# Convolution results written over their inputs, and the inverse square root as a product of polynomials

## The chip, the core and the metric

The kernel runs on one core of one Trainium2 chip. The metric is the device time of one execution in microseconds. All data are 32-bit floats.

## What is computed

The reference has two layers on x of shape (4 images, 64 channels, 256, 256). The first is a long convolution with an implicit filter: per channel, a filter that is the outer product of two vectors of 256 taps, made by a small network of sines; the FFTs of size 512 make it a causal (not cyclic) convolution. Since the filter separates, it equals a Toeplitz product along the rows and one along the columns. The second layer takes the covariance of a ninth of the pixels over the channels, computes its inverse square root by five Newton-Schulz steps, and applies it to the centred image.

```
k = einsum('ijk,imk->ijmk', hx, hy)            # per channel: outer product of two 256-tap filters
y = irfft2(rfft2(x, 512) * rfft2(k, 512))[:256, :256] + x * bias

x1  = y as (64 channels, 4*256*256 pixels)
x1s = x1[:, ::9]
mean = mean(x1s, axis=-1)
cov = x1s @ x1s.T / n + 0.01 * I
Y, Z = cov / norm(cov), I
for _ in range(5):
    T = 0.5 * (3 I - Z @ Y);  Y = Y @ T;  Z = T @ Z
out = Z / sqrt(norm(cov)) @ (x1 - mean)
```

## The kernel before

*Set-up.* The filter taps are made on the chip in the first 20 us and written to DRAM (`g_d`). Toeplitz matrices are read back from there with overlapping rows into tiles `toep`, three buffers, one for each group of 8 channels.

*The convolution.* A step is a group of 8 channels (g) of one image (n); there are 32 steps. Steps 0 to 23 go through groups 0 to 5 with the four images inside; steps 24 to 31 go through the images, with groups 6 and 7 inside, so that image 0 is complete after step 25, image 1 after step 27, and so on. A step has four items of two channels (c = 0, 2, 4, 6). Each call of `group` (L381) interleaves the second Toeplitz product of an item with the first of the item two places later, four PSUM banks of eight; ScalarE moves the first product's result to SBUF (L396), VectorE makes `y = x * bias + second product` (L399) into a tile of its own, and SP stores it to DRAM (`store`, L407, 512 KB a store, rows of 1 KB). One call takes TensorE some 4.6 us; the calls are chained through two items (`pending`).

*Tiles.* One pool, `big`, holds three tiles of x (tag "in") and three of y (tag "out"), 2 MB each (16 KB per partition). x of step i+2 is loaded during step i (L103), one item's piece after each call of `group`.

*Sampling.* For every finished y tile, nine predicated copies on VectorE (L313) pick every ninth pixel into `samp[n]`, three copies after each call of `group`. The last half tile is picked by TensorE with selection matrices (`pack_by_pe`, L289). `covariance(n)` (L321) multiplies the samples of an image; that of image n-1 is taken in the middle of step (g=7, n), the last one after the convolution.

*The order.* The instructions of all engines stand in the order in which the program issues them (a manual schedule); a queue is served in that order. In particular, SP issues x loads, Toeplitz blocks, stores of y and reloads of y one after another, and each waits for what it needs while the others stand behind it.

*The second pass.* The whitening matrix W is applied to y, which comes back from DRAM in 32 pieces of 128 partitions x 4096 (2 MB). A piece holds 64 channels of two images (`pieces`, L338; `y_d` has 128 rows of one pair of images). A reload (`load_y`, L346) needs a free tile: 13 tiles become homes (L341): three of `toep`, four of `samp`, three of x and three of y. Eight reloads are issued inside the convolution, at the places that `early` (L372) names by step and item, five after it. A later piece waits until its home's earlier piece has been written out. Per 1024 columns: four matmuls (L585), two evictions on ScalarE (L590) and two on VectorE (L593) that add the shift, and an output DMA issued by POOL (L598), 2 MB each but for the first and last two pieces, which go in quarters.

*The inverse root.* Between the passes, on 64x64 matrices (L478 to L567): the norm as a square root on ScalarE with one correction step, then five rounds of ZY, T, YT, TZ. Each product goes through PSUM and is copied by VectorE (L505) or ScalarE (L550). At the end come the scaling, a product that doubles the matrix onto 128 partitions, and the shift `-W mean`.

Of the kernel before, what the change touches and what calls it, by code (L numbers as in the profile page):

```python
# [37 lines left out]
F32 = mybir.dt.float32  # L38
# [27 lines left out]
def conv_whiten_kernel(ctx: ExitStack, tc: tile.TileContext, a: dict, out: bass.AP):  # L66
# [4 lines left out]
    big = ctx.enter_context(tc.tile_pool(name="big", bufs=3))  # L71
# [6 lines left out]
    y_d = [dram.tile([2 * C, PIX], F32, tag=f"y{v}", name=f"y_d{v}") for v in range(NB // 2)]  # L78
# [5 lines left out]
    scratch = big.tile([P, 16, L], F32, tag="out", name="scratch")  # L84
# [14 lines left out]
    def new_x(g, n):  # L99
        return big.tile([P, CG, H2, L], F32, tag="in", name=f"x_{g}_{n}")  # L100

# [9 lines left out]
    loaded = {s: new_x(*s) for s in steps[:2]}  # L111
    for c in range(0, CG, 2):
        load_x(loaded[steps[0]], *steps[0], c)
# [147 lines left out]
    def half_group(item, which):  # L261

        g, n, c, xt, yt, o1s = item
# [11 lines left out]
        for m in range(H2):  # L275
            for u in range(2):
# [5 lines left out]
                else:  # L282
                    ch = g * CG + c + u
                    nc.vector.scalar_tensor_tensor(  # L284
                        yt[:, c + u, m], xt[:, c + u, m], bias[:, ch : ch + 1], ps,
# [35 lines left out]
    def covariance(n):  # L321
# [16 lines left out]
    pieces = [(v, q) for v in range(NB // 2) for q in range(PIX // FP)]  # L338
# [3 lines left out]
        {"t": (tpool, "toep"), "s": (spool, "samp"), "i": (big, "in"), "o": (big, "out")}[k]  # L342
        for k in "tssioitsoitos"
    ]

    def load_y(i):  # L346

        v, q = pieces[i]
        pool, tag = homes[i % len(homes)]
        t = pool.tile([P, FP], F32, tag=tag, name=f"yi_{v}_{q}")  # L350
        nc.sync.dma_start(out=t, in_=y_d[v][:, q * FP : (q + 1) * FP])
        return t
# [4 lines left out]
    loaded_x, loaded = loaded, {}  # L357
# [14 lines left out]
    early = {(28, 4): 1, (28, 6): 1, (29, 6): 1, (30, 4): 1, (31, 2): 1, (31, 4): 1, (31, 6): 2}  # L372
# [8 lines left out]
    def group(first, second):  # L381

        units = []
        g1, n1, c1, x1, _, o1s1 = first
        g2, n2, c2, x2, y2, o1s2 = second
# [7 lines left out]
        for u in range(2):  # L393
            o1 = o1pool.tile([P, H2, L], F32, tag="o1", name=f"o1_{g1}_{n1}_{c1 + u}")
            for to, fr in ((slice(0, HP), slice(HP, P)), (slice(HP, P), slice(0, HP))):
# [4 lines left out]
                y2[:, c2 + u], x2[:, c2 + u], bias[:, ch : ch + 1], units[u][1][0],  # L400
# [6 lines left out]
    def store(second):  # L407
        g, n, c, _, yt, _ = second
        last = (g, n) == steps[-1]
        row = n % 2 * C + g * CG + c  # L410
        nc.sync.dma_start(
            out=y_d[n // 2][row : row + 2, :].rearrange(
                "c (b p w) -> p (c b) w", p=P, w=L
            ),
            in_=yt[:, c : c + 2].rearrange("p c b w -> p (c b) w"),
        )
        if last and c == CG // 2 - 2 or not last and c == CG - 2:
            todo.extend(pack_ops(g, n, yt, slice(0, c + 2)))

    engines = mybir.EngineType  # L420
    with tc.manual_schedule(
# [7 lines left out]
        for c in range(0, CG, 2):  # L429
            load_x(loaded_x[steps[1]], *steps[1], c)  # L430
        for i, (g, n) in enumerate(steps):
            xt = loaded_x.pop((g, n))
            yt = big.tile([P, CG, H2, L], F32, tag="out", name=f"y_{g}_{n}")
            for c in range(0, CG, 2):
                item = (g, n, c, xt, yt, [])
# [7 lines left out]
                if i == 0 and c == 6:  # L443
# [3 lines left out]
                    twice = const.tile([C, 2, C], F32, tag="twice", name="twice")  # L447
                    for u in range(2):
                        nc.vector.tensor_copy(twice[:, u], ident[0:C, 0:C])

                part = (c - 2) // 2 % 4
                to = i + 2 if c else i + 1
                if to < len(steps) and to > 1:
                    if part == 0:
                        loaded_x[steps[to]] = new_x(*steps[to])
                    load_x(loaded_x[steps[to]], *steps[to], 2 * part)
# [8 lines left out]
        g, n, c, xt, yt, _ = pending[0]  # L465
# [4 lines left out]

        pack()
        pack_by_pe(g, n, yt, slice(CG // 2, CG))
# [3 lines left out]


    spare = {}  # L478
    for i in range(2):
        t = o1pool.tile([P, H2 * L], F32, tag="o1", name=f"chain{i}")  # L480
        for j in range(5):
            spare[5 * i + j] = t[0:C, 72 * j + 72 : 72 * j + 72 + C]
    ones = spare[9]
    nc.gpsimd.memset(ones, 1.0)  # L484
    i15 = spare[8]
    nc.vector.tensor_scalar(i15, ident[0:C, 0:C], 1.5, None, ALU.mult)
    spots = {"A": [0], "sq": [1], "Y": [2, 3], "T": [4, 5], "Z": [6, 7], "Zs": [1]}

    columns = [t[0:C, 440 + k : 441 + k] for k in range(H2 * L - 440)]

    def column():
        return columns.pop()

    def matrix(tag):
        spots[tag].append(spots[tag].pop(0))
        return spare[spots[tag][-1]]

    def product(lhsT, rhs, name):
        p = psA.tile([lhsT.shape[1], rhs.shape[1]], F32, tag="psA", name=name)
        nc.tensor.matmul(p, lhsT=lhsT, rhs=rhs, start=True, stop=True)  # L500
        return p

    def keep(p, name, tag):
        t = matrix(tag)
        nc.vector.tensor_copy(t, p)  # L505
        return t


    pd = product(fold, cov, "pd")
    A = matrix("A")  # L510
    nc.vector.scalar_tensor_tensor(A, ident[0:C, 0:C], EPS, pd[:, 0:C], ALU.mult, ALU.add)
    mean = column()
    nc.scalar.copy(mean, pd[:, C : C + 1])

    def root(v, name):

        s0 = column()
        nc.scalar.activation(s0, v, AF.Sqrt)  # L518
        r = column()
        nc.vector.reciprocal(r, s0)  # L520
        s1 = column()
# [135 lines left out]
```

## Time and profile before

| | us |
|---|---|
| median of 3 runs (917.23 to 919.46) | 918.35 |
| the profiled execution | 917.19 |
| its span, first to last instruction | 915.2 |
| TensorE busy | 789.1 (86%) |
| VectorE busy | 658.2 (72%) |
| ScalarE busy | 479.2 (52%) |
| POOL busy | 31.7 (3%) |

DMA moves 285.57 MB: x in, y out, y in and the result out are 67 MB each, the rest are Toeplitz blocks and small inputs. The mean granted TensorE clock was 0.946 of full speed. The page cuts the span into 40 slices of 22.9 us; a digit in a row is the busy share of a slice in tenths. The durations in the groups are of one instruction in ns; "idle before" is the time in which the engine stood still just before instructions of that group, with what ended it.

### The profile page before, as it was taken

How to read it: one execution, taken by the hardware profiler on the slowest of the kernel's cores; microseconds unless marked ns; L12 is line 12 of the kernel's file. 1: busy time of each engine (PE TensorE's matmuls, PEld its weight loads, DVE VectorE, ACT ScalarE, POOL GpSimd, SP SyncE). 2: the span in 40 equal slices, each digit the busy share in tenths (PEclk: the TensorE clock that was granted, in tenths of full speed). 3: DMA queues.
4: the chain of work that ended last, by engine and by line, in shares of the span. 5: the costliest groups of instructions: out<-in, count | busy, mean ns of one | idle time of the engine just before them, and what ended most of it. 6: DMA issues, size and time to landing. Idle time of an engine off the chain costs nothing.

```text
span 915.2 us, 27979 instructions
## 1 busy us (share of the span) xinstructions
PE 789.1 (86%) x11876; PEld 633.3 (69%) x11876; DVE 658.2 (72%) x882; ACT 479.2 (52%) x791; POOL 31.7 (3%) x71
## 2 busy tenths in 40 slices
PE   8999999999999999999999999997877777765500
PEld 7999999999999999999999999996311111111100
DVE  3468776877687768786878666867599999986500
ACT  2545454545454545454545444540498888866400
POOL 3000000000000000000000000000110000000010
PEclk9999999999999999999999999998699999987655
DMA  4988888798888888889997769989999999999998
GB/s 152 304 282 260 248 259 271 229 273 261 246 263 261 246 260 260 257 249 279 278 274 232 236 192 364 326 276 406 416 404 431 428 430 430 430 430 430 429 433 347
DMA packets 115499, 285.57 MB, mean 312 GB/s; under 512 B 6925, under 2 KB 89264, under 8 KB 107696
## 3 DMA queue, kind: packets, MB, share of 16 engines
q1 hardware_dynamic: 108176, 216.08, 71.0%
q0 software_dynamic: 6336, 67.11, 17.3%
q8 instruction: 94, 1.54, 0.7%
q10 hardware_dynamic: 864, 0.60, 0.2%
q14 instruction: 29, 0.24, 0.1%
HBM read 149.35 MB, written 134.42 MB: 310 GB/s over the span
## 4 chain that ended last, share of the span: by engine, by line
PE 68%; issue 15%; DVE 13%; DMA 1%; POOL 1%; ACT 0%; ACTq 0%; POOLq 0%; DVEq 0%
PE p L215 63%; DVE yi L593 12%; PE pc L327 2%; PE ph L247 1%; PE pk L295 1%; DMA mask<-in_mask_dram 1%; POOL pick L131 1%; PE po L585 1%; POOL out_dram L598 0%; DMA toep<-g_d 0%; DVE y L284 0%; PE ZY L500 0%; PE YT L500 0%; ACT L518 0%; DMA g_d<-scratch 0%
## 5 line engine op out<-in xcount | busy, mean ns | idle before, releaser
L215 PE MATMUL p<-toep,o 64*64 64x64 f32 (+3 forms) x5040 | 578.5, 284 | 0.2 <-issue 0.2
L215 PE MATMUL p<-toep,x 64*64 64x64 f32 (+3 forms) x5040 | 578.5, 284 | 0.1
L215 PEld LDWEIGHTS p<-toep,x 64*128 64x128 f32 (+1 forms) x5040 | 533.9, 166 | 23.4 <-issue 0.3
L215 PEld LDWEIGHTS p<-toep,o 64*128 64x128 f32 (+1 forms) x5040 | 535.2, 166 | 10.7 <-issue 0.4
L396 ACT COPY o<-p 64x512 f32<-64x512 f32 x504 | 292.4, 580 | 297.7 <-PE p L215 289.9
L313 DVE COPY_PREDICATED samp<-mask,y 128x448 f32<-128x448 int32 (+3 forms) x288 | 281.2, 976 | 6.6
L399 DVE SCALAR_TENSOR_TENSOR y<-x,bias,p 128x512 f32<-128x512 f32 x252 | 177.4, 743 | 138.7 <-PE p L215 138.1
L593 DVE TENSOR_SCALAR yi<-po,shift 64x512 f32<-64x512 f32 x256 | 192.0, 750 | 24.8 <-PE po L585 18.5
L585 PE MATMUL po<-yi,W 64*64 64x512 f32 x1024 | 152.4, 668 | 62.4 <-DVE yi L593 39.4
L590 ACT ACTIVATE yi<-po,shift 64x512 f32<-64x512 f32 x256 | 174.9, 683 | 43.9 <-PE po L585 36.8
L585 PEld LDWEIGHTS po<-yi,W 64*64 64x64 f32 x1024 | 36.8, 145 | 177.2 <-DVE yi L593 123.3
L598 POOL DMA_DIRECT2D out_dram<-yi x44 | 23.6, 537 | 263.2 <-DMA out_dram<-yi 115.4
L484 POOL MEMSET chain<- 64x64 f32 x1 | 0.1, 144 | 603.2 <-PE ph L247 603.2
L327 PEld LDWEIGHTS pc<-samp 128*64 128x64 f32 x464 | 14.3, 137 | 1.8 <-issue 1.0
L327 PE MATMUL pc<-samp 128*64 128x65 f32 x464 | 14.9, 223 | 0.4 <-ACT samp L304 0.4
L150 PE MATMUL busy<-idle 128*128 128x128 f32 x94 | 13.0, 301 | 0.0
L150 PEld LDWEIGHTS busy<-idle 128*128 128x128 f32 x94 | 12.4, 216 | 0.2 <-issue 0.2
L281 DVE COPY o<-ph 64x256 f32<-64x256 f32 x8 | 3.4, 421 | 9.1 <-PE ph L247 8.9
L295 PE MATMUL pk<-y,pick 128*128 128x112 f32 (+1 forms) x36 | 7.7, 388 | 2.6 <-DVE y L284 2.6
L335 DVE SCALAR_TENSOR_TENSOR cov<-pc,cov 128x65 f32<-128x65 f32 x4 | 0.9, 227 | 12.1 <-PE pc L327 12.1
L295 PEld LDWEIGHTS pk<-y,pick 128*128 128x128 f32 x36 | 7.2, 258 | 2.8 <-issue 2.7
L281 ACT COPY o<-ph 64x256 f32<-64x256 f32 x8 | 2.9, 367 | 10.0 <-PE ph L247 9.9
(81 smaller groups left out, 80.3 us busy)
## 6 DMA issues: line engine op xcount, KB each, us to landing
x<-in_x_dram SPq DMA_DIRECT2D x128, 512.0 KB, 5.5
y_d<-y SPq DMA_DIRECT2D x128, 512.0 KB, 4.2
yi<-y_d SPq DMA_DIRECT2D x32, 2048.0 KB, 16.4
out_dram<-yi POOLq DMA_DIRECT2D x28, 2048.0 KB, 44.3
out_dram<-yi POOLq DMA_DIRECT2D x16, 512.0 KB, 9.8
toep<-g_d SPq DMA_DIRECT2D x29, 256.0 KB, 6.6
toep<-g_d SPq DMA_DIRECT2D x29, 192.0 KB, 5.8
toep<-g_d SPq DMA_DIRECT2D x6, 128.0 KB, 3.2
```

Source lines behind the costliest of these rows:

```text
L131: nc.gpsimd.tensor_scalar(pick[:, s, :], ident, rows[:, s : s + 1], None, ALU.mult)
L150: nc.tensor.matmul(p, lhsT=idle[:, 0:P], rhs=idle[:, P : 2 * P], start=True, stop=True)
L215: mm = nc.tensor.matmul(ps[q : q + w, m, HP * k : L], lhsT=src[parts, k // 2, m * P + q : m * P + q + w], rhs=t[parts, : stop : -1] if k e ...
L295: nc.tensor.matmul(pk[:, b, :, 0:nj], lhsT=pick[:, (s - b) % STEP, :], rhs=yt[:, cs, b, s : s + STEP * (nj - 1) + 1 : STEP], start=(s == 0 ...
L313: nc.vector.copy_predicated(dst, m, src)
L327: nc.tensor.matmul(pc[half], lhsT=samp[n][:, b, j, 0:C], rhs=samp[n][:, b, j, :], start=(b == 0 and j < 2), stop=(b == H2 - 1 and j >= NJ ...
L396: nc.scalar.copy(o1[to], units[u][0][0][fr])
L399: nc.vector.scalar_tensor_tensor(y2[:, c2 + u], x2[:, c2 + u], bias[:, ch : ch + 1], units[u][1][0], ALU.mult, ALU.add,)
L585: nc.tensor.matmul(po[u][halves[k]], lhsT=W[halves[u]], rhs=yt[halves[u], cols[k]], start=True, stop=True,)
L590: nc.scalar.activation(yt[halves[0], cols[k]], po[0][halves[k]], AF.Identity, bias=shift[halves[k]])
L593: nc.vector.tensor_scalar(yt[halves[1], cols[k]], po[1][halves[k]], shift[halves[k]], None, ALU.add)
L598: nc.gpsimd.dma_start(out=o[:, end - part : end], in_=yt[:, end - part : end])
```

## The change

1. y is written over x (`scalar_tensor_tensor` with the same tile as input and output). Four fixed tiles (`x_tiles`) take the steps in turn, by `place_of`; from step 27 on only three are used. Two more tiles (`epool`) are free after the set-up. There are still 13 homes: two extra, four of x, three of `toep`, four of `samp`.
2. A tile can be loaded anew only when its y has been stored and sampled. x of step i+2 is loaded during step i up to step 24, from item c=0 on (before: from c=2 on); in step 25 nothing is loaded; from step 26 on, step i loads x of step i+1.
3. `y_d` has one tensor for each image, with rows of half a channel: (2 halves x 64 channels) x 32768. A store of an item becomes two stores of 256 KB. A piece is of one image, with both halves of the channels on the 128 partitions; the result has the same layout, and the host puts the axes in order.
4. Nine reloads are issued inside the convolution, from step 26 on; four after it.
5. The inverse root: with A the covariance and r = 1/norm(A), T0 = 1.5 I - 0.5 r A; the following factors are worked out from powers of A (A squared and cubed on TensorE while the norm is made), then per round Q = T T, M' = Q M, T' = 1.5 I - 0.5 M', and Z is multiplied up on the side with the mean as a 65th column. The last factor is made twice side by side, so that the last product comes out on 128 partitions and gives W and the shift at once. The square-root table is loaded by a dummy instruction in step 0.
6. Fill matmuls (`spin`): six after the last convolution product, seven while the norm is made, two after each of the products of the rounds.

```diff
-    big = ctx.enter_context(tc.tile_pool(name="big", bufs=3))
+    xpool = ctx.enter_context(tc.tile_pool(name="xpool", bufs=4))
+    epool = ctx.enter_context(tc.tile_pool(name="epool", bufs=2))
-    y_d = [dram.tile([2 * C, PIX], F32, tag=f"y{v}", name=f"y_d{v}") for v in range(NB // 2)]
+    y_d = [dram.tile([H2 * C, PIX // H2], F32, tag=f"y{n}", name=f"y_d{n}") for n in range(NB)]
...
+    x_tiles = {
+        u: xpool.tile([P, CG, H2, L], F32, tag="in", name=f"x{u}") for u in (3, 2, 0, 1)
+    }
+    def place_of(i):
+        return i % 4 if i < 27 else i % 3
...
-    pieces = [(v, q) for v in range(NB // 2) for q in range(PIX // FP)]
+    pieces = [(n, q) for n in range(NB) for q in range(PIX // H2 // FP)]
-        for k in "tssioitsoitos"
+        for k in "eeitssistiits"
...
-    early = {(28, 4): 1, (28, 6): 1, (29, 6): 1, (30, 4): 1, (31, 2): 1, (31, 4): 1, (31, 6): 2}
+    early = {
+        (26, 4): 1, (26, 6): 1, (27, 0): 1, (27, 2): 1, (27, 6): 1, (29, 6): 1, (31, 0): 1, (31, 4): 2
+    }
...
             nc.vector.scalar_tensor_tensor(
-                y2[:, c2 + u], x2[:, c2 + u], bias[:, ch : ch + 1], units[u][1][0],
+                x2[:, c2 + u], x2[:, c2 + u], bias[:, ch : ch + 1], units[u][1][0],
                 ALU.mult, ALU.add,
             )
...
-        row = n % 2 * C + g * CG + c
-        nc.sync.dma_start(
-            out=y_d[n // 2][row : row + 2, :].rearrange("c (b p w) -> p (c b) w", p=P, w=L),
-            in_=yt[:, c : c + 2].rearrange("p c b w -> p (c b) w"),
-        )
+        for b in range(H2):
+            row = b * C + g * CG + c
+            nc.sync.dma_start(
+                out=y_d[n][row : row + 2, :].rearrange("c (p w) -> p c w", w=L),
+                in_=yt[:, c : c + 2, b],
+            )
...
-                part = (c - 2) // 2 % 4
-                to = i + 2 if c else i + 1
-                if to < len(steps) and to > 1:
-                    if part == 0:
-                        loaded_x[steps[to]] = new_x(*steps[to])
-                    load_x(loaded_x[steps[to]], *steps[to], 2 * part)
+                to = i + 2 if i < 25 else i + 1
+                if i != 25 and to < len(steps):
+                    load_x(x_tiles[place_of(to)], *steps[to], c)
...
+    def spin(times):
+        p = psA.tile([P, P], F32, tag="psA", name=f"spin{len(spins)}")
+        spins.append(p)
+        for _ in range(times):
+            nc.tensor.matmul(p, lhsT=ident, rhs=ident, start=True, stop=True)
...
+    def whitening(i15, ones):
+        one_i15 = i15[:, 0]
+        pd = product(fold, cov, "pd")
+        A = place(C, rows=C)
+        nc.vector.scalar_tensor_tensor(A, ident[0:C, 0:C], EPS, pd[:, 0:C], ALU.mult, ALU.add)
...
+        pa2 = product(A, A, "pa2")
+        pn = product(ones, sq, "pn")
...
+        nc.vector.tensor_reduce(ssq, pn, AX.X, ALU.add)
+        nc.scalar.activation(s0, ssq, AF.Sqrt)
...
+        pa3 = product(A2a, A, "pa3")
+        spin(7)
...
+        nc.vector.scalar_tensor_tensor(U, pa3, rn_c, A2b, ALU.mult, ALU.add)
+        nc.vector.scalar_tensor_tensor(V, U, rn_c, A1b, ALU.mult, ALU.add)
+        T, M, Z = Ts[0], Ms[0], Zs[0]
+        nc.vector.scalar_tensor_tensor(T, V, rn_c, one_i15, ALU.mult, ALU.add)
+        nc.vector.tensor_scalar(M, V, rn_c, -2.0, ALU.mult, ALU.mult)
...
+        for k in range(1, N_ITER - 1):
+            pq = product(T, T, f"pq{k}")
+            if before is not None:
+                next_z(k - 1, before)
+            spin(2)
+            Q = Qs[k % 2]
+            nc.vector.tensor_copy(Q, pq)
+            pm = product(Q, M, f"pm_{k}")
...
+            if k < N_ITER - 2:
+                spin(2)
+                T, M = Ts[k % 2], Ms[k % 2]
+                nc.vector.scalar_tensor_tensor(T, pm, -0.5, one_i15, ALU.mult, ALU.add)
+                nc.vector.tensor_copy(M, pm)
...
+            else:
+                next_z(k, T)
+                spin(2)
...
+        pw = product(T, Z, "pw")
+        W = place(C)
+        nc.vector.tensor_scalar(W, pw[:, 0:C], rs, None, ALU.mult)
+        nc.scalar.activation(shift, pw[:, C : C + 1], AF.Copy, scale=nrs)
...
+        spin(6)
         pack()
...
+        W, shift = whitening(i15, ones)
```

`place` hands out columns of the tiles of the pool `o1`, and `product` is a matmul into a PSUM tile of its own.

## The prediction

> **What bounds the kernel now.** I read the page first: the 40 slices, then the costliest groups.
>
> ```profile
> span 915.2 us, 27979 instructions
> ...
> PEclk9999999999999999999999999998699999987655
> DMA  4988888798888888889997769989999999999998
> GB/s 152 304 282 260 248 259 271 229 273 261 246 263 261 246 260 260 257 249 279 278 274 232 236 192 364 326 276 406 416 404 431 428 430 430 430 430 430 429 433 347
> ...
> L215 PE MATMUL p<-toep,x 64*64 64x64 f32 (+3 forms) x5040 | 578.5, 284 | 0.1
> ```
>
> A slice is 22.9 us. Up to slice 26 (some 620 us) TensorE runs the Toeplitz products back to back: the row's last field, its idle time, is 0.1 us. Here DMA moves some 250 GB/s and has room. From slice 27 on, DMA stands at 430 GB/s, a ceiling. The second view is the table of stretches (columns: PE, PEld, DVE, ACT, POOL busy, granted clock, DMA share, GB/s).
>
> ```profile
> 512.00:545.00 33.00, 33.00 (x614) 30.84 (x613) 23.88 (x30) 15.56 (x28) 0.00 (x0) 1.00 0.65 207
> 554.10:572.90 18.80, 18.80 (x410) 17.69 (x408) 11.02 (x15) 7.12 (x13) 0.00 (x0) 1.00 0.99 390
> 604.00:616.00 12.00, 12.00 (x248) 11.39 (x244) 5.08 (x7) 3.70 (x7) 0.00 (x0) 1.00 0.89 289
> 616.00:912.50 296.50, 176.65 (x1273) 57.75 (x1270) 212.48 (x310) 179.29 (x268) 23.78 (x45) 0.84 1.00 422
> 621.70:625.10 3.40, 0.83 (x6) 0.58 (x5) 3.40 (x8) 0.00 (x0) 0.00 (x0) 1.00 1.13 448
> 625.10:628.50 3.40, 3.40 (x18) 3.40 (x17) 3.23 (x6) 0.00 (x0) 0.00 (x0) 0.51 0.99 424
> ```
>
> The fourth line decides: from 616 us to 912.5 us, DMA is at share 1.00, with no hole where the inverse root is computed (632 to 650 us). Third, the timeline there:
>
> ```profile
> 624.49 7.65 PE L295 MATMUL pk<-y,pick 128*128 128x116 f32 x36 [2.57 <-DVE y L284]
> ...
> 632.54 3.71 PE L327 MATMUL pc<-samp 128*64 128x65 f32 x116 [0.40 <-ACT samp L304]
> ...
> 650.10 6.49 PE L585 MATMUL po<-yi,W 64*64 64x512 f32 x29
> ...
> 654.34 0.73 POOL L598 DMA_DIRECT2D out_dram<-yi  x1 [35.48 <-PE po L585]
> ```
>
> The first output leaves at 654.3 us, yet DMA is busy throughout: five reloads of y (2 MB each) are issued between 625.65 and 639.4 us, and queue. So two things set the end: when TensorE finishes the convolution, and how many bytes are left for DMA then. The inverse root is covered by DMA.
>
> Last, the SP queue and its landing times (last column of the second fence: us from issue to landing; one issue per line, in the order 509.26, 549.70, 554.93, 558.83, 563.45):
>
> ```profile
> 509.26 0.50 SPq L103 DMA_DIRECT2D x<-in_x_dram  x1
> ...
> 549.70 0.50 SPq L103 DMA_DIRECT2D x<-in_x_dram  x1
> 550.30 0.87 SPq L351 DMA_DIRECT2D yi<-y_d  x1
> ...
> 554.93 0.43 SPq L351 DMA_DIRECT2D yi<-y_d  x1
> ```
>
> ```profile
> x<-in_x_dram SPq DMA_DIRECT2D x1, 512.0 KB, 5.7
> ...
> x<-in_x_dram SPq DMA_DIRECT2D x1, 512.0 KB, 5.8
> ...
> yi<-y_d SPq DMA_DIRECT2D x1, 2048.0 KB, 13.9
> ...
> x<-in_x_dram SPq DMA_DIRECT2D x1, 512.0 KB, 12.6
> ...
> x<-in_x_dram SPq DMA_DIRECT2D x1, 512.0 KB, 10.8
> ```
>
> Landings come in order of issue: 555.5, 568.8, 571.4, 574.3 us. The queue is first in, first out, so an x load behind two reloads takes 12.6 us in place of 5.8.
>
> **The change, part by part.**
>
> *1. y in the place of x; pieces of one image.* The 128x512 multiply-add (743 ns) writes x's tile; sizes are unchanged, so 0. Two tiles are freed, and image 0 is complete after step 25, so reloads start at step 26 in place of 28. From the store times (a step of four groups lasts some 18.6 us) the reloads issued inside the convolution move from 550, 555, 577, 590, 604, 613, 617, 617 us to about 510, 514, 519, 523, 536, 577, 600, 613, 613. At 613 us, where DMA saturates, seven have landed and two are issued, against five and one: two reloads ahead. 2 x 2.097 MB at 430 GB/s = **-9.75 us** of saturated tail. That holds only if the queue stays fed until outputs start: nine reloads, the stores and the last four (issued at about 625.7, 632, 632, 636 us, behind the packing, the pick products and the covariance) at 5.3 us each keep DMA busy to about 651 us.
>
> *2. What the early reloads push aside.* From step 25 on, x is loaded one step ahead in place of two (three tiles are left), and four reloads are put into four consecutive groups. The x load behind them for step 28, c=4 has the bytes of 4 reloads, 4 stores and 4 x loads after the x load of 509.26 (landed 515.0): 12.58 MB. The rate of such a mix is in the trace: between the x landings 555.5 and 574.3 lie 2 reloads, 3 stores, 3 x loads, 7.34 MB in 18.8 us, 390 GB/s. It lands at 515.0 + 32.2 = 547.2; TensorE wants it at 543.5 (the store of the group before, 544.34, less 0.82, the distance from a group's end to its store at 557.59/558.41). **3.6 us late.** The load for step 29, c=0 comes 4.19 MB (10.7 us) later, at 557.9, wanted at 552.8: 5.1 late, of which 3.6 is already paid. A 3.6 us gap also costs clock (below): 3.4 us at half speed, 1.7 us. Together the larger of 5.1 and 3.6+1.7: **+5.3 us** on the convolution's end, and the whole tail shifts with it. Here the Trainium skill weighs against the change: "HBM Reference", Specifications (TRN2), gives 358 GB/s per core, though its text says that a core streaming alone does better. With 358 the delay would be 9.0 us, and the change worth nothing; the trace has 390 in just this mix, so I take that.
>
> *3. Stores in two halves, loads behind the packing.* 128 stores of 512 KB become 256 of 256 KB, each with the same 1 KB runs. SP spends 0.38 us an issue, so some 0.4 us more per group of 4.6 us, of which it uses 1 to 2. In a backed-up queue a 512 KB store adds some 1.4 us; I take the halves at 0.7. A load at c=0 now waits for the last packing of its tile (up to 3 x 0.98 us after the multiply-adds); a Toeplitz block or a store queued behind it on SP waits as long. Below step 26 the cover is two steps: 0. If halves were slower, DMA's room (share 0.65 from 512 to 545 us) covers it, except in the crowded steps, where 0.2 us each would add some 2 us to part 2; a gain has no room, as TensorE has no idle time there.
>
> *4. The inverse root.* Before: covariance in at 636.5, W at 649.3, first output 654.3, with the clock at 0.50 from 638.7. After: six fill matmuls (0.28 us each, the row of L150) shorten the idle 2.57 us to 0.9; the pick products then run at full clock, but the last packings on DVE (to 631.5 us) allow only 0.7 us of gain. A square-root table load (1.28 us, about 0.5 of it exposed) moves to step 0, where ACT idles 1.5 us per group. Four rounds of three products become three of two squarings in the critical chain, but TensorE also runs the fills in order: a round is 2 products + 2 x 2 fills + side products, about 1.9 us at full clock. W at some 645.7, first output at 648.4: 6 us earlier. **Yet part 1's queue is busy to 651 us, so it is worth 0.** It is needed: with the old chain, DMA would idle some 3 us. The clock: "TensorE: Matmul & The Clock Gate", Part 1, puts the drop to half after an idle window of about 3.4 us. The trace dropped it after an idle gap of only 2.57 us (rows 621.7 and 625.1, with 0.83 us of TensorE work in the first). By the page the old gap did no harm and the fills there buy nothing; by the row they hold the clock. I follow the row. If the clock were half all the same, the fills (0.55 us each) would stretch the rounds to 3.7 us and the first output to some 656: +5 us.
>
> *5. Restart of the tail.* Between the end of the backlog and the first reload into a freed tile, DMA has only outputs (2.1 MB per 6.19 us, 339 GB/s). Before it ran at 349 to 419 GB/s there; I take **+0.5 us**.
>
> **Sum:** -9.75 + 5.3 + 0.5 = -4.0 us. The profiled execution was 917.19 us (span 915.2 and 2.0 around it), 1.2 under the median of 918.35; the difference is set against the median: **914.4 us**, a span of about 911.3.
>
> **The rivals.**
> - *The x loads come in time.* At the tail's 430 GB/s the two loads are 0.8 and 1.2 us late: -9.75 + 1.2 + 0.5, 910.3 us. For it: 430 is what the engines can do. Against it: 390 with 1 KB stores mixed in.
> - *Slower: the reloads starve TensorE in steps 28 and 29.* Five reloads, six stores and six x loads, 16.8 MB, must pass from 515.0 on. Delay passes 11.1 us (-9.75 + 11.1 + 0.5, the 0.2% bound) when they run under 344 GB/s; at 330 the delay is 13.1 us, 922.2 us. For it: a lone reload takes 9.2 to 9.6 us, and the stretch 604 to 616 gave 289 GB/s. Against it: 390 with two in the queue.
> - *The clock falls in the chain* (part 4): +1.0 us in all, 919.4, no change.
> - *The shorter chain is what counts* (if DMA were not full): -4.0 would be -6 or better. Against it: share 1.00 from 616 us.
>
> **How the numbers follow.** A measurement here tells about 0.2% (1.8 us) from no change. Main case 0.40 (911 to 917), no stall 0.22, cold chain or a delay of 7.5 to 11 us 0.17, starved 0.16, something unseen that costs 0.05. Range for 8 in 10: 908.0 (close to no stall) to 921.5. Faster 0.62, same 0.17, slower 0.21.
>
> **What would show it.** TensorE's Toeplitz products should wait for x in steps 28 to 29 (some 5 us, DMA as releaser), and the granted clock may dip at 547 us; before step 26, nothing. The first output should leave near 653 us (648.4 + 5.3), with DMA at share 1.0 from about 618 us on, and 13 reloads issued by then. Wrong: no wait for x (then near 910), a wait over 11 us, DMA idle before the first output, or clock 0.5 in the chain.

## The result, and the profile after

| | before | after |
|---|---|---|
| median | 917.17 us (915.12 to 919.46) | 917.69 us (915.40 to 920.36) |
| span of the profiled execution | 915.2 us | 915.7 us |
| end of the last Toeplitz product | 621.9 us | 628.3 us |
| first output issued | 654.34 us | 656.88 us |
| mean granted clock | 0.946 | 0.957 |

The ratio is 0.9997, with a 95% interval of 0.9988 to 1.0007: no change that can be measured. (The 917.17 us are of 12 runs beside those of the changed kernel; the 918.35 us from which the forecast started were of three.) The forecast was 914.4 us; the time lies inside the range, but "faster" was the likeliest outcome and did not come. That the range holds is partly luck: an unchanged time was forecast only with a clock of 0.5 in the chain or a delay of 7.5 to 11 us, and neither came.

The rows of the page of the changed kernel that answer to those shown of before:

```profile
span 915.7 us, 28266 instructions
...
PEclk9999999999999999999999999999999999996655
DMA  4988778788788788878984899789999999999998
GB/s 154 298 282 273 253 243 262 256 258 259 258 261 264 237 266 265 262 236 267 291 277 138 302 412 340 252 286 357 379 379 432 426 432 429 429 432 429 429 433 340
...
L220 PE MATMUL p<-toep,x 64*64 64x64 f32 (+3 forms) x5040 | 580.8, 285 | 3.8 <-DMA x<-in_x_dram 3.1
```

Three things are new. In slices 22 and 23 (counted from 0; 504 to 550 us) DMA moves 302 and 412 GB/s where it moved 236 and 192: the early reloads. In slice 21, just before, it moves 138 GB/s in place of 232: in step 25 no x is loaded. And the Toeplitz products now have idle time, 3.1 us of it ended by a load of x. In slices 27 to 29 (618 to 687 us) the GB/s row reads 357, 379, 379 where it read 406, 416, 404: DMA has holes where it was full.

The stall, in the timeline of TensorE and then in the table of stretches (columns: PE, PEld, DVE, ACT, POOL busy, granted clock, DMA share, GB/s):

```profile
540.99 0.24 PE L220 MATMUL p<-toep,x 64*64 64x64 f32 x1 [0.34 <-DMA x<-in_x_dram]
548.53 0.45 PE L220 MATMUL p<-toep,x 64*128 64x256 f32 x1 [2.74 <-DMA x<-in_x_dram]
```

```profile
541.00:548.00 7.00, 4.80 (x78) 4.19 (x78) 5.11 (x7) 4.11 (x8) 0.00 (x0) 1.00 1.00 393
548.30:549.70 1.40, 1.17 (x9) 1.07 (x11) 0.00 (x0) 0.00 (x0) 0.00 (x0) 0.99 1.17 469
549.70:553.10 3.40, 3.40 (x22) 3.12 (x20) 0.00 (x0) 0.00 (x0) 0.00 (x0) 0.50 1.03 439
553.10:560.00 6.90, 6.90 (x139) 6.51 (x137) 4.90 (x6) 3.26 (x6) 0.00 (x0) 1.00 1.01 386
```

An x load that came 2.74 us late, then 3.4 us at clock 0.50, half of which (1.7 us) is my estimate of the further cost. The first multiply-add of each group stands 1.5 us later than before at step 27, c=2, 2.1 us at c=6, and 7.2 us one group on: 5.7 us in all, 5.1 of them in one place. At the end of the convolution 6.4 us are left; some 1.4 us of that is spread over the first 26 steps, and not every profile shows it.

Now the tail. For each kernel the stretch in which DMA can run out of work, up to 668 us, with parts of it, and the stretch from 616 us to the end of the span. Before, then after:

```profile
616.00:632.00 16.00, 13.43 (x99) 12.55 (x96) 15.15 (x26) 1.41 (x3) 0.14 (x1) 0.89 1.01 399
656.00:668.00 12.00, 11.90 (x85) 3.44 (x77) 11.62 (x17) 11.68 (x18) 3.70 (x7) 1.00 1.00 399
616.00:668.00 52.00, 42.02 (x358) 26.21 (x355) 35.50 (x75) 19.22 (x34) 4.61 (x9) 0.80 1.01 410
616.00:915.20 299.20, 176.65 (x1273) 57.75 (x1270) 212.48 (x310) 179.29 (x268) 23.78 (x45) 0.83 0.99 419
```

```profile
616.00:632.00 16.00, 14.97 (x213) 13.83 (x210) 14.25 (x21) 4.64 (x8) 0.20 (x1) 1.00 0.88 322
648.00:656.00 8.00, 7.62 (x64) 5.02 (x65) 3.38 (x14) 2.38 (x7) 0.00 (x0) 1.00 1.01 430
656.00:668.00 12.00, 11.86 (x78) 3.34 (x70) 11.62 (x17) 11.66 (x19) 4.20 (x8) 1.00 0.77 291
616.00:668.00 52.00, 48.96 (x526) 35.42 (x522) 38.68 (x79) 19.99 (x40) 4.39 (x9) 1.00 0.92 358
616.00:915.70 299.70, 185.13 (x1452) 66.22 (x1448) 217.87 (x317) 181.92 (x276) 23.90 (x45) 0.87 0.98 409
```

These lines give the whole balance. Rate times length of the longer stretch is what DMA still had to move at 616 us: 125.4 MB before, 122.6 MB after, so 2.8 MB less, worth 6.5 us at 430 GB/s. Rate under 430 from 616 to 668 us is what it failed to move: 20 x 52 = 1.0 MB (2.4 us) before, 72 x 52 = 3.7 MB (8.7 us) after. So 6.5 us of head start were won and 6.3 us of holes were added. The added holes lie in two places of about the same size. From 616 to 632 us, while the delayed convolution still runs (to 628.3 us), the rate is 322 GB/s against 399: 1.2 MB, 2.9 us. From 656 us on, where the first outputs leave and DMA has little else, it is 291 against 399: 1.3 MB, 3.0 us. In between DMA is nearly full, at 430 GB/s from 648 to 656 us, up to just before the first output (656.88 us).

The chain between the passes, in the timeline of TensorE of the changed kernel:

```profile
630.98 7.60 PE L300 MATMUL pk<-x,pick 128*128 128x116 f32 x36 [1.03 <-DVE x L289]
638.98 3.71 PE L332 MATMUL pc<-samp 128*64 128x65 f32 x116 [0.40 <-ACT samp L309]
643.01 0.33 PE L448 MATMUL pd<-cov,fold 128*64 128x65 f32 x2 [0.32 <-DVE cov L340]
...
652.64 0.43 PE L448 MATMUL pw<-chain,chain 64*128 64x65 f32 x2
653.45 7.00 PE L622 MATMUL po<-yi,chain 64*64 64x512 f32 x56 [0.38 <-DVE chain L541]
```

From the convolution's end to the first output it takes 28.5 us where before it took 32.4. The clock stayed at 1.00 there, so the new root did what it says; it started 6.4 us later.

How far the backlog of reloads reaches past the first output is read from the issue of the last of the 13 reloads, its time to landing, and the issue of the first reload into a freed tile (first and third line from the timeline of SP, the second from the list of transfers). Before, then after:

```profile
638.08 1.31 SPq L351 DMA_DIRECT2D yi<-y_d  x1
yi<-y_d SPq DMA_DIRECT2D x1, 2048.0 KB, 25.5
668.16 0.32 SPq L351 DMA_DIRECT2D yi<-y_d  x1
```

```profile
642.73 0.32 SPq L356 DMA_DIRECT2D yi<-y_d  x1
yi<-y_d SPq DMA_DIRECT2D x1, 2048.0 KB, 15.8
664.80 0.32 SPq L356 DMA_DIRECT2D yi<-y_d  x1
```

Before, the last reload landed at 663.6 us, 9.3 us after the first output was issued. After, it landed at 658.5 us, 1.6 us after the first output. I call this the lead of the backlog.

### The profile page after: what moved, and what is told of

Its sections match the earlier page's. It is cut to its first block, busy times and chain, and to the rows that moved or that the text cites. A ratio compares the mean times of both kernels' runs of the same rounds, so it can differ in the third digit from the quotient of the medians.

```text
span 915.7 us, 28266 instructions
## 1 busy us (share of the span) xinstructions
PE 793.6 (87%) x11922; PEld 637.6 (70%) x11922; DVE 658.8 (72%) x882; ACT 480.1 (52%) x796; POOL 31.9 (3%) x71
## 4 chain that ended last, share of the span: by engine, by line
PE 68%; DVE 17%; issue 7%; DMA 5%; ACT 1%; POOL 0%; POOLq 0%; DVEq 0%; ACTq 0%; SPq 0%
PE p L220 62%; DVE yi L630 16%; DMA yi<-y_d 3%; PE pc L332 2%; DMA x<-in_x_dram 1%; PE ph L252 1%; PE po L622 1%; PE pk L300 1%; PE spin L433 0%; ACT yi L627 0%; POOL out_dram L635 0%; DMA toep<-g_d 0%; DVE x L289 0%; DVE scratch L168 0%; ACT scratch L164 0%
## 5 line engine op out<-in xcount | busy, mean ns | idle before, releaser
L318 DVE COPY_PREDICATED samp<-mask,x 128x448 f32<-128x448 int32 (+3 forms) x288 | 281.2, 976 | 6.7
L406 DVE SCALAR_TENSOR_TENSOR x<-x,bias,p 128x512 f32<-128x512 f32 x252 | 177.4, 743 | 145.1 <-PE p L220 144.6
L622 PE MATMUL po<-yi,chain 64*64 64x512 f32 x1024 | 150.6, 655 | 60.7 <-DVE yi L630 42.3
L622 PEld LDWEIGHTS po<-yi,chain 64*64 64x64 f32 x1024 | 35.1, 141 | 175.2 <-DVE yi L630 131.6
L300 PE MATMUL pk<-x,pick 128*128 128x112 f32 (+1 forms) x36 | 7.6, 385 | 1.0 <-DVE x L289 1.0
L300 PEld LDWEIGHTS pk<-x,pick 128*128 128x128 f32 x36 | 7.1, 206 | 1.3 <-issue 1.2
```

Of the source, the lines that this page charges most:

```text
L300: nc.tensor.matmul(pk[:, b, :, 0:nj], lhsT=pick[:, (s - b) % STEP, :], rhs=yt[:, cs, b, s : s + STEP * (nj - 1) + 1 : STEP], start=(s == 0 ...
L318: nc.vector.copy_predicated(dst, m, src)
L406: nc.vector.scalar_tensor_tensor(x2[:, c2 + u], x2[:, c2 + u], bias[:, ch : ch + 1], units[u][1][0], ALU.mult, ALU.add,)
L622: nc.tensor.matmul(po[u][halves[k]], lhsT=W[halves[u]], rhs=yt[halves[u], cols[k]], start=True, stop=True,)
```

## The experiments

Theory: the head start of the reloads is real (some 9.7 us), but it is lost in two places: a stall of TensorE, because x loads queue behind four reloads, and a DMA queue that runs dry as the first outputs leave, so that the inverse root, hidden before, is on the path. Rivals: the stores in two halves or the writing over x cost time; the fill matmuls cost or save time; the tail restarts badly because the first reload into a freed tile comes late.

The times below stand against runs of the kernel before on the same chip (medians 917.75, 917.75 and 917.38 us in the three batches).

### Reloads spread out

At most one reload in two groups, otherwise the changed kernel; still nine inside the convolution.

```diff
-        (26, 4): 1, (26, 6): 1, (27, 0): 1, (27, 2): 1, (27, 6): 1, (29, 6): 1, (31, 0): 1, (31, 4): 2
+        (26, 4): 1, (27, 0): 1, (27, 4): 1, (28, 0): 1, (28, 4): 1, (29, 6): 1, (31, 0): 1, (31, 4): 2
```

> The changed kernel with the same nine early reloads, the first five moved apart: after (26,4), (27,0), (27,4), (28,0), (28,4) in place of (26,4), (26,6), (27,0), (27,2), (27,6). Theory (x loads stand behind a run of four reloads in the first-in-first-out queue): TensorE's wait for x in steps 28 and 29 (2.7 us and the half clock after it) goes, the convolution ends near 623.5 us in place of 628.3, the first output leaves near 652 in place of 656.9, and the time falls by 4 to 5 us against before (ratio 0.995). Rival 1 (the one-step lead, not the reloads, makes x late): the wait stays. Rival 2 (the lost time is DMA's at the start of the tail, so TensorE's wait costs nothing): the wait goes and the time stays at 1.000.

Measured: 911.19 us (910.92 to 912.86), ratio 0.9936 (0.9922 to 0.9949): 5.8 us faster than before by the ratio. The stretches of this kernel:

```profile
500.00:560.00 60.00, 60.00 (x1098) 56.39 (x1096) 43.76 (x54) 29.10 (x51) 0.00 (x0) 1.00 0.95 348
...
616.00:632.00 16.00, 15.00 (x114) 14.21 (x110) 15.56 (x27) 1.74 (x3) 0.20 (x1) 1.00 1.00 386
648.00:656.00 8.00, 8.00 (x62) 2.39 (x54) 7.29 (x10) 7.37 (x11) 2.33 (x4) 1.00 0.75 308
650.70:653.00 2.30, 2.30 (x21) 0.70 (x14) 2.24 (x4) 2.24 (x4) 1.24 (x2) 1.00 0.48 191
656.00:668.00 12.00, 10.28 (x66) 2.50 (x64) 11.63 (x17) 11.68 (x18) 2.44 (x5) 1.00 0.94 342
...
616.00:668.00 52.00, 47.41 (x428) 30.56 (x424) 40.11 (x82) 23.14 (x43) 4.98 (x10) 1.00 0.95 377
616.00:909.30 293.30, 178.54 (x1322) 60.71 (x1318) 213.24 (x312) 179.08 (x271) 23.91 (x45) 0.87 0.98 413
```

TensorE is busy for 60.00 of 60 us and the clock is 1.00: no stall, although x is loaded one step ahead here too. The convolution ends at 622.2 us, the first output leaves at 650.67. So the stall cost the changed kernel some 6 us: 5.6 by the two ratios, 6.5 by the medians (917.69 less 911.19), where the interval of this ratio alone is 2.5 us wide. At 616 us DMA had 121.1 MB left, 4.2 MB less than before: the two reloads of head start, with nothing taken off. Yet only 5.8 us of their 9.8 arrived, because the holes are 53 x 52 = 2.8 MB (6.4 us) against 2.4 us before: -9.8 + 4.0 = -5.8, and the spans differ by -5.9 (909.3 against 915.2). Of the two places, the first is nearly gone (386 GB/s from 616 to 632 us); the holes lie from 648 us on.

### Reloads at the old places

The changed kernel with the reload places of before: what do the layout, the half stores, the loads behind the packing and the new root bring without the head start?

```diff
-    early = {
-        (26, 4): 1, (26, 6): 1, (27, 0): 1, (27, 2): 1, (27, 6): 1, (29, 6): 1, (31, 0): 1, (31, 4): 2
-    }
+    early = {(28, 4): 1, (28, 6): 1, (29, 6): 1, (30, 4): 1, (31, 2): 1, (31, 4): 1, (31, 6): 2}
```

> The changed kernel with the early reloads at the places they had before: (28,4), (28,6), (29,6), (30,4), (31,2), (31,4) and two at (31,6). Theory: no wait for x, the convolution ends near 623 us; the tail has the bytes it had before, DMA is full through the inverse root, so the time is that of before within 1 us (1.000 to 1.001). If writing y over x or the stores in halves cost something by themselves, this run shows it: over 1.002. Rival (the shorter inverse root counts): 3 us less, 0.997.

Measured: 917.69 us (915.75 to 919.45), ratio 0.9999 (0.999 to 1.0007). No wait for x, the first output at 649.51 us (4.8 us earlier than before), and in its stretches DMA is full all through:

```profile
632.00:656.00 24.00, 22.53 (x253) 13.85 (x248) 13.75 (x40) 10.57 (x24) 2.73 (x5) 1.00 1.02 424
656.00:668.00 12.00, 9.88 (x69) 2.32 (x64) 11.64 (x16) 11.68 (x18) 2.27 (x5) 1.00 1.01 418
```

So half stores, the place of y and the later loads, together with the new root, change nothing that can be measured, and an earlier first output is worth nothing here. Parts of under a microsecond that cancel are not excluded.

### The new root alone, and the old root in the changed kernel

Two crossed kernels: the kernel before with the new root and the fills, and the changed kernel with the old root and no fills.

```diff
 # in the kernel before
-    (norm, five rounds of ZY, T, YT, TZ, doubling, shift)
+    spin(6); ...; W, shift = whitening(i15, ones)
 # in the changed kernel: the reverse
```

> The kernel before with only the new inverse root and its fill matmuls (parts 5 and 6 of the change). Theory: DMA is full from 616 us to the end, so the first output leaves some 4 us earlier (650 in place of 654.3) and the time stays: 1.000 within 0.1%. Rival (the inverse root is on the path): 3 to 4 us less, 0.996.

> The changed kernel with the old inverse root and no fills. Theory: here DMA ran dry at 656 us (217 GB/s from 656 to 660, 0.77 of its time from 656 to 668), so the later first output (about 660.7 in place of 656.9, by the 32.4 us from the end of the convolution to the first output before, against 28.5) is paid in full: 3 to 4 us slower than the changed kernel, 1.004 of before. Rival (covered by the reloads, as I predicted): 0.

Measured: the new root alone 916.99 us, ratio 0.9991 (0.9983 to 0.9999); the old root in the changed kernel 921.79 us, ratio 1.0044 (1.0031 to 1.0056). In the one the first output moved by -4.4 us (649.97) and the time by -0.8; in the other by +4.5 us (661.42) and the time by +4.1. The second kernel's tail:

```profile
656.00:668.00 12.00, 11.76 (x78) 4.22 (x78) 9.04 (x15) 8.57 (x13) 2.83 (x5) 0.84 0.49 197
```

At share 0.49, DMA idles for half of this stretch: the last of the 13 reloads landed at 659.7 us, before the first output was even issued. The same chain was hidden in the kernel before and is exposed in the changed one.

### No fills

```diff
     def spin(times):
-        p = psA.tile([P, P], F32, tag="psA", name=f"spin{len(spins)}")
-        spins.append(p)
-        for _ in range(times):
-            nc.tensor.matmul(p, lhsT=ident, rhs=ident, start=True, stop=True)
+        return
```

> The changed kernel without any fill matmul. Theory: the fills are what holds the granted clock at 1.0 in the chain; without them it falls to about 0.50 between the end of the convolution and the first output matmuls. The pick products take 7.6 us all the same (they took 7.65 us before with 3.4 us of them at half clock, and 7.60 us in the changed kernel at full clock), so they are not bound by the clock. The chain from covariance to W (10.4 us with fills) loses the waits behind fills and gains some 0.2 us a product: between 10 and 12 us. The first output moves by 0 to +1.5 us, and since DMA ran dry there, the time by about as much: 917.5 to 919, ratio 1.000 to 1.002. Rival (the prediction's cold chain): half clock costs 5 us, ratio 1.005 or more. Second rival: the fills cost more than the clock brings, ratio 0.998 or less.

Measured: 917.73 us, ratio 1.0 (0.9991 to 1.0008), the same as with fills. The stretches of the chain (pick products; chain to W; first outputs):

```profile
632.00:640.00 8.00, 7.60 (x38) 7.23 (x37) 6.60 (x13) 0.27 (x1) 0.00 (x0) 0.62 1.00 371
...
644.00:653.60 9.60, 5.47 (x30) 3.86 (x30) 5.12 (x27) 1.82 (x10) 0.00 (x0) 0.73 1.01 429
653.60:657.90 4.30, 4.26 (x20) 1.30 (x24) 1.98 (x3) 2.15 (x4) 0.00 (x0) 0.50 0.83 354
```

The clock does fall. The pick products take 7.91 us (7.60 with fills), and the first output matmuls take 4.3 us up to the first output (3.4 with fills). But the products of the rounds no longer stand behind fills: from `pd` to `pw` it takes 8.57 us (644.00 to 652.57) against 9.63. From the end of the convolution to the first output: 28.9 us without fills, 28.5 with. They hold the clock and give it back as queueing on TensorE.

### Quarter reloads into the first freed tiles

The first two reloads into freed tiles, in four parts, so that each waits for its own quarter's output alone; once in the changed kernel, once with spread reloads.

```diff
-            loaded[i + len(homes)] = load_y(i + len(homes))
+            if i < 2:
+                m, r = pieces[i + len(homes)]
+                for w in range(4):
+                    nc.sync.dma_start(
+                        out=yt[:, w * 1024 : (w + 1) * 1024],
+                        in_=y_d[m][:, r * FP + w * 1024 : r * FP + (w + 1) * 1024],
+                    )
+                loaded[i + len(homes)] = yt
+            else:
+                loaded[i + len(homes)] = load_y(i + len(homes))
```

> The changed kernel, with the first two reloads into freed tiles cut in four, so that each quarter waits for the output of its own quarter alone. Theory: from 656 to 668 us DMA lost 1.3 MB (291 GB/s against 399 before) because the first whole reload waits for four outputs; the quarters start after the first of them and fill some 0.7 to 1.3 MB of it: -1.6 to -3.0 us, ratio 0.9967 to 0.9983, 390 GB/s or more from 656 to 668 us. Rival: the tail is not bound by DMA there but by how soon outputs leave (VectorE and ScalarE are busy 97% in that stretch), so that bytes moved early only queue later: 0, ratio 0.9995 to 1.0005. Second rival: quarters on the SP queue delay each other and the whole reloads behind them: slower by up to 1 us.

> The kernel with spread reloads (911.2 us) and the first two reloads into freed tiles cut in four. Theory: there DMA moved 342 GB/s from 656 to 668 us and 368 from 640 to 656; the quarters fill the first of the two: -1.0 to -2.4 us against 911.2, 908.8 to 910.2 us, ratio 0.9910 to 0.9925. Rival (outputs bound the tail): 911 us, ratio 0.9936.

Measured: 916.84 us, ratio 0.9995 (0.9985 to 1.0004), and 912.15 us, ratio 0.9938 (0.9924 to 0.9953). Both miss. With spread reloads and quarters:

```profile
648.00:656.00 8.00, 8.00 (x65) 2.45 (x57) 6.80 (x10) 6.90 (x11) 2.10 (x4) 1.00 0.72 267
656.00:668.00 12.00, 10.04 (x65) 2.52 (x66) 11.59 (x16) 11.65 (x18) 2.37 (x5) 1.00 1.00 386
```

The quarters did start earlier (3.2 us after the first output, at 654.28 us, where the whole reload came 7.9 us after it) and filled the second stretch: 386 against 342 GB/s. The first stretch was no better, 267 against 308, so that over 616 to 668 us the rate is 379 against 377. Most of the hole (163 x 8 = 1.3 MB of 1.8 MB from 648 to 668 us) lies in the first stretch, where DMA waits for the first output and then has little but outputs; reloads issued from 654.28 us on come too late for it. The rivals of both expectations, with no gain from the quarters (0.9995 to 1.0005, and 0.9936), have the numbers right; their reason, that the pace of the outputs and not DMA sets the end there, was not tested.

### One fill in place of two

The kernel just above, with `spin(1)` for each `spin(2)`.

```diff
-            spin(2)
+            spin(1)
```

> As the one before, with one fill matmul in place of two after each product of the rounds. Theory: the products that stand behind the fills start up to 0.3 us earlier, five or six times: first output 1 to 1.5 us earlier, clock still 1.0; DMA had room there, so 0 to -1.2 us against the kernel before it. Rival: one fill is too few, the clock falls to 0.5 in the rounds, first output no earlier, time the same or up to 1 us more.

Measured: 911.97 us, ratio 0.9937 (0.9923 to 0.9951): no difference. From `pd` to `pw` it took 8.39 us in place of 9.63, as expected. But then the clock fell in the first output matmuls, which took 4.3 us in place of 3.4:

```profile
641.00:650.00 9.00, 7.84 (x60) 6.08 (x58) 5.12 (x27) 1.87 (x11) 0.00 (x0) 0.98 1.00 424
650.00:653.40 3.40, 3.40 (x20) 1.16 (x24) 1.25 (x2) 1.53 (x3) 0.00 (x0) 0.55 1.03 439
```

Most of the gain of the chain (1.2 us) went into these 3.4 us at clock 0.55 (0.9 us). Both sides of the expectation were right in part, and they cancelled to 0.3 us; the clock fell behind the rounds, not in them.

### One reload moved by one group

The prediction's arithmetic of the queue, tested: the x load that came late (step 28, c=4) stands behind three reloads in place of four.

```diff
-        (26, 4): 1, (26, 6): 1, (27, 0): 1, (27, 2): 1, (27, 6): 1, (29, 6): 1, (31, 0): 1, (31, 4): 2
+        (26, 4): 1, (26, 6): 1, (27, 0): 1, (27, 4): 1, (27, 6): 1, (29, 6): 1, (31, 0): 1, (31, 4): 2
```

> The changed kernel with one reload moved by one group, from step 27 c=2 to c=4, so that the x load of step 28 c=4 (issued 535.36, landed 548.4, waited for by 2.74 us) stands behind three reloads in place of four. By the prediction's arithmetic a reload is 5.4 us at 390 GB/s: that load comes in time, and the next ones, behind four, take over the stall. Theory: the following load (step 28 c=6) is then 1 to 3 us late: 2 to 4 us are won back of the 6.4: 914 to 916, ratio 0.996 to 0.998. Rival 1: the stall only moves (no gain): 917.5, ratio 0.9995 or more. Rival 2: three in a row are harmless, the stall is gone: 911 to 912, ratio 0.993 to 0.9945.

Measured: 917.77 us, ratio 1.0003 (0.9993 to 1.0013): nothing is won. Its waits of TensorE between 540 and 575 us, and the stretches:

```profile
PE p L220 <- DMA x<-in_x_dram: 3.3, 2, 2.6
```

```profile
552.00:556.00 4.00, 2.73 (x30) 2.19 (x26) 3.27 (x5) 1.96 (x4) 0.00 (x0) 1.00 0.97 372
556.00:560.00 4.00, 2.65 (x17) 2.68 (x19) 2.37 (x3) 0.36 (x1) 0.00 (x0) 0.79 1.06 398
560.00:564.00 4.00, 4.00 (x84) 3.88 (x85) 0.25 (x1) 0.15 (x1) 0.00 (x0) 0.79 0.95 362
```

The stall only moved: the jump of the multiply-adds against before stands two groups later (1.8 us at step 28, c=2, 6.8 us at c=4; in the changed kernel 2.1 to 7.2 us at c=0), 5.0 us in place of 5.1, with the dip of the clock behind it. The next two x loads stand behind the fourth and the fifth reload, and the prediction's order of bytes has the second of them, for step 29, c=0, late too. Behind three reloads the load came in time; room for the others has to be made by distance, as the spread kernel does.

### Part of the sampling left out

The pick products and the covariance of the last image left out, in three kernels: with spread reloads, as changed, and with the reloads at the old places. This was to bring the first output forward by some 12 us and so price the chain.

```diff
-        pack_by_pe(g, n, yt, slice(CG // 2, CG))
-        covariance(NB - 1)
```

> The kernel with spread reloads, without the pick products and the covariance of the last image (left out: the samples of the last half tile and of image 3 are missing from the whitening matrix); all else, the four last reloads too, is as there. Theory: with spread reloads DMA had 4.15 MB less to move at 616 us than before (9.65 us), but lost 7.0 us to holes up to 912 us against 3.7 before, 4.7 of them between 648 and 668 us, while it waited for the first outputs. With W some 12 us earlier (first output near 638.5) the backlog covers the whole chain and the holes from 648 to 668 go: -4 to -5 us against 911.2, 906 to 907.5, ratio 0.988 to 0.989. Rival: the holes are not due to the late first output (SP's queue, or the order of small and large transfers); then they stay and the time falls by less than 1 us, ratio 0.9925 to 0.994.

> The changed kernel, with the same part left out (pick products and covariance of the last image). Theory: its hole from 656 to 668 us (291 GB/s, 1.67 MB under 430) goes, as the first output leaves near 644.5 us: -3.5 to -4.5 us, 913 to 914, ratio 0.995 to 0.9965. The prediction's own view (the queue covers the inverse root): 0, ratio 0.9995 to 1.0005.

> The changed kernel with its reloads at the places of before (917.7 us), with the same part left out. Theory: there DMA was at share 1.01 through the whole chain (the backlog covers it), lost bytes from 616 to 700 us are 0.9 MB; the first output 12 us earlier is worth at most 1 us: 916.7 to 917.7, ratio 0.9989 to 1.0. Rival: the first output sets the end in every kernel: -4 us or more, ratio 0.996 or less.

Measured: 909.34 us, ratio 0.9912 (0.9896 to 0.9928); 914.94 us, ratio 0.9977 (0.9965 to 0.9988); 917.36 us, ratio 1.0002 (0.9993 to 1.0012). The edit did not do what it was meant to do. With spread reloads, TensorE then stood for one long wait:

```profile
PE pa L448 <- DVE chain L461: 8.0, 1, 8.0
```

VectorE still had its packings to do, and the chain's first operation (L461) stands behind them; in that wait the clock fell (0.61 from 628 to 640 us). So the first output came only 3.4 us earlier (647.32), and the time fell by 1.9 us (2.2 by the ratios, whose intervals just touch). The DMA stretch from 616 to 668 us reads 394 GB/s against 377:

```profile
632.00:656.00 24.00, 23.03 (x148) 12.67 (x148) 15.97 (x45) 12.71 (x27) 3.39 (x6) 0.89 1.01 424
...
616.00:668.00 52.00, 41.00 (x298) 22.60 (x294) 43.11 (x85) 26.70 (x48) 5.19 (x10) 0.90 1.00 394
```

That is 17 x 52 = 0.9 MB, 2.1 us, as much as the time fell. With the old places the first output came even later (652.85 against 649.51 us, at the lower clock), and the time did not change; but the landing of the last reload moved as far, so the lead of the backlog stayed (13.7 us against 13.2). In the kernel in the middle the time is 2.8 us under the changed kernel's (1.8 by the ratios), but its runs spread from 912.7 to 920.5 us and the profiled one, of 918.5 us, lies near their upper end (first output 657.96 us), so that its profile doesn't show where the median gained.

## Where the prediction was right, and the step that failed

The sum was -9.75 (head start) + 5.3 (stall) + 0.5 (restart) = -4.0 us. In the same terms the runs give -9.8, +5.6 to 6.5 and +4.0 us, together between -0.2 and +0.7; measured were -0.3 by the ratio and +0.5 by the medians. The first and the last term are read from the kernel with spread reloads, the stall is the difference between that kernel and the changed one. So nearly all that the forecast missed lies in the restart.

*Part 1, the head start: right.* 4.2 MB (9.8 us) less to move at 616 us, in the kernel with spread reloads, against 4.19 MB and 9.75 us predicted. In the changed kernel the stall leaves 2.8 MB of it.

*Part 2, the stall: right in its mechanism, and in size as far as can be told.* Which x load would be late, behind which bytes, and the dip of the clock came as worked out: 3.6 us late was forecast and 2.74 + 0.34 us came; the convolution slipped by 5.7 us there, against 5.3. Moving one reload moved the stall and won nothing. The rate was right too: 393 GB/s from 541 to 548 us. The 358 GB/s of the Trainium skill ("HBM Reference", Specifications (TRN2)) did not weigh against the change, as the prediction had it: the page gives them as a core's share while both cores of a pair stream, and this kernel has one core at work. The rivals on this part fell: "in time" by the wait, "starved" by its size.

*Part 3, half stores, y over x, loads behind the packing: right, 0 within what can be measured.* The kernel with the old places is 0.9999 of before.

*Parts 4 and 5: this step failed.* "Part 1's queue is busy to 651 us, so it is worth 0" took a queue that lasts until the first output as enough, and part 5 put the restart behind it at 0.5 us. In the kernel without a stall the times came close to the forecast: DMA was full to about 650 us (forecast 651), the first output left at 650.67 (forecast 648.4), and the last reload landed 1.6 us after it. Yet the holes cost 4.0 us more than before. Until the first reload into a freed tile, issued 7.9 us after the first output, DMA has little but outputs: 191 GB/s from 650.7 to 653 us, 342 from 656 to 668. The 349 to 419 GB/s that the prediction read for this phase in the kernel before were the rate of a covered restart: there the backlog had a lead of 9.3 us, and the outputs queued up with it. The reloads of the head start are that cover. Two reloads landed early are 9.75 us less of backlog to hide the chain and the restart behind, while the first output moved by only 3.7 us (654.34 to 650.67). The cause stands on pairs of kernels, in which a shift of the first output has different prices:

| pair | lead of the backlog | shift of the first output | change of the time |
|---|---|---|---|
| before, with the new root | 9.3, then 13.9 us | -4.4 us | -0.8 us |
| old places, part of the sampling left out | 13.2, then 13.7 us | +3.3 us | -0.3 us |
| changed kernel, with the old root | 1.6, then -1.7 us | +4.5 us | +4.1 us |
| spread, part of the sampling left out | 1.6, then 5.6 us | -3.4 us | -1.9 us |

With a lead of 9 us and more, an earlier first output brings next to nothing (first row). With one under 6 us, a microsecond of chain costs between a half and a whole one (third and fourth row). The second row agrees but is no test, since the lead did not change. The forecast had noted that the new root "is needed" and that with the old chain DMA would idle some 3 us (the old chain cost 4.1). The rival "the shorter chain is what counts" was right in its mechanism, but not as it was put: the chain counts in the changed kernel because the cover is gone, which takes from the head start and adds nothing to -4. I take leads and shifts from one profile of each kernel, and in these profiles the convolution of like kernels ends up to 3.6 us apart, so the slopes are rough.

*The clock in the chain.* The fills hold it at 1.00, as forecast, but this is worth nothing: without them the time is the same, because each fill also stands in front of a product. The 0.7 us hoped for from the pick products did not come either: they take 7.60 us at full clock, as against 7.65 with 3.4 us of half clock. The Trainium skill ("TensorE: Matmul & The Clock Gate", Part 1) puts the drop after an idle window of some 3.4 us; here a gap of 2.74 us in the convolution was followed by 3.4 us at half clock, as one of 2.57 us was before. The row, not the page, was the right guide.

*The first output* was forecast near 653 us and came at 656.88: 648.4 + 5.3 against 650.67 + 6.2. So without the stall it was 2.3 us later than forecast. Some 1.2 us of that is the second fill: `pd` to `pw` takes 9.63 us with two fills after each product, 8.39 with one. The rest was not traced.

The best version of these runs is the spread one: 911.19 us, 0.9936 of before. Quarters and one fill on top of it brought nothing that can be measured.

## What to carry to other kernels

A transfer moved ahead of a saturated stretch buys its full time there only if the stretch stays saturated; the same bytes were hiding whatever ran beside them. So after every such step ask three things: when the backlog now ends, when the first work that feeds DMA again can leave, and when the transfers that wait for this work can start. Here a backlog that ended 1.6 us after the first output left holes worth 4 us more than one that ended 9.3 us after it. Price a microsecond of what lies between at a half to a whole one, not at zero. Early transfers in a first-in, first-out queue are best put apart, with the loads that the critical engine waits for between them: four in consecutive groups cost some 6 us, the same number at half the density none.

## What the runs showed that I had not expected

- The strided pick products are nearly independent of the clock: 7.60 us at 1.00, 7.65 us with 3.4 us of half clock, 7.91 us at a mean of 0.62. The output matmuls up to the first output are not: 3.4 against 4.3 us.
- Filling a hole in DMA with more eager reloads raised the rate from 656 to 668 us from 342 to 386 GB/s and yet left the sum to 668 us where it was (377 and 379 GB/s).
- SP itself was held by the crowded reloads: in the changed kernel the fourth was issued at 530.81 us, 8 us after the third, and SP's own waits between 510 and 552 us name a reload's landing as what ended 6.6 us of them.
